# Moving keys, bias adds and value loads within the rounds of a decoder block kernel

## The chip, the core and the metric

The kernel runs on one core of one Trainium2 chip. A core has a matrix engine (TensorE, PE in the profile; its weight loads are shown as PEld), a vector engine (VectorE, DVE), a scalar engine (ScalarE, ACT), a general engine (GpSimd, POOL), and a queue engine (SyncE, SP) that here issues most of the transfers between device memory and on-chip memory. Each engine takes its instructions in the order of its own program and waits at an instruction until what it needs is there. The metric is the device time of one execution in microseconds; lower is better.

## The reference, cut to what matters

The kernel computes one decoder layer on 32 sequences ("blocks" in the code) of 256 tokens and 256 features, in float32, with a normalisation behind each of three parts:

```python
x = layernorm(x + self_attention(x))       # 16 heads, causal, keys and values of 72 latent columns
x = layernorm(x + cross_attention(x, ctx)) # 16 heads of 64, 120 context rows
x = layernorm(x + experts(x) + shared(x))  # 16 experts, each takes its best 32 tokens of a block

# self_attention
kv = x @ latent_w + latent_b                       # (256, 72): keys and values at once
q  = x @ Wd_w[h] + Wd_b[h]                         # (256, 72) for each head h
y  = softmax(causal(q @ kv.T / 4)) @ kv            # for each head
return concat(y) @ out_w + out_b
```

## The kernel before

**Stages.** Attention and the expert scores are computed in rounds, one per block, and fill the first 2100 us; the experts and the shared part follow and fill the rest. Round n (functions `first_half(n)` and `second_half(n)`) works on several blocks at once: the self attention scores of block n, the end of the self attention of block n - 1, cross attention of blocks n - 1 and n - 2, the last part of block n - 3, and the preparation of block n + 1 (load, transpose, keys, first queries, values). Block 0 is prepared in an opening part and run in `first_round()`.

**Quarters.** The 16 heads are worked in four groups of four, so a round has four quarters, each opened by `scores(n, g)`. For a group, TensorE computes scores into four accumulation banks; VectorE adds the causal mask (L479) and takes the maxima (L486); ACT takes exponentials and their sums (L493); VectorE inverts the sums (L503); POOL multiplies (L504); VectorE transposes in squares of 32 (L538, `turn`). After two groups `weigh(n, half)` multiplies with the values (pz, L564), the result z goes through device memory into zT (L586 to L592), and `latent_out` multiplies with the output weights (po) in the second quarter of the next round.

**The second quarter of round n** ends the self attention of block n - 1: `latent_out(n - 1)`, the moments and `norm_x1(n - 1)` (VectorE, L173, in two steps of 128 tokens), `turn_x1(n - 1)` (four transposes on TensorE, px1T, and one copy on VectorE, x1T, L195), then the cross queries of x1 (pqx). Between them stand `turn_x(n + 1)`, the third queries `queries(n, 2)` (pq), a part of the cross keys (pkx) in odd rounds or of the cross values (pvx) in even ones, and `keys(n + 1)`: two matmuls (pk), a copy with bias on ACT (kT, L377) and one on VectorE (kD, L378). In every fourth round, from round 6 on, `score` turns the gate's logits (pgT) ahead of pqx.

**The bias of the output projection** is added to x itself before the residual sum, by two adds on POOL (L366) at the end of `turn_x`. They read x after the transposes of x; their result is read by `latent_out` of that block, more than a round later.

**Values.** `values(n + 1)`, in the last quarter, transposes kT (pv), copies it (v) and writes it to device memory (vd). `place_values(n)`, in the second quarter of the next round, reads it back four times, one copy for each group of 32 partitions, into the one tile `vals`. That tile is read by both `weigh` of a block, the second of which stands in the first quarter of the round after; so the new values wait until `weigh(n - 1, 1)` is done.

**What sets the order.** The scope `tc.manual_schedule(engines=...)` keeps the order in which the code records instructions for the engines that it names: all engines in the opening part; TensorE, ACT and SP in `first_round`; TensorE, ACT, VectorE and POOL in the rounds. The engines that it does not name, SP in the rounds above all, are ordered by the scheduler, from the recorded order and its own estimates. Tiles of a pool with `bufs=k` rotate through k buffers, and a new tile waits until the last readers of the old one are done. Accumulation banks of the tag "r" rotate through six (`BUFS`), in the order in which they are asked for, whatever engine empties them; `cross_scores` has two banks of its own.

Of the kernel before, what the change touches and what calls it, by code (L numbers as in the profile page):

```python
# [26 lines left out]
P = 128  # L27
# [5 lines left out]
def decoder_kernel(  # L33
# [210 lines left out]

    kr = kp.tile([P, NG, T], F32, name="kr")
    nc.gpsimd.memset(kr, 0.0)

    vals = wp.tile([P, RB, TC, L], F32, name="vals")
    nc.gpsimd.memset(gw_sb, 0.0)

    xsms = [[cw.tile([P, HG, P], F32, name=f"xsm_{o}_{k}") for k in range(2)] for o in range(2)]
# [109 lines left out]
    def turn_x(s):  # L361
        st = states[s]
        st["xT"] = sp.tile([P, DC, T], F32, tag="xT", name=f"xT_{st['nm']}")
        transposed(st["xT"], (st["x"][:, 0, :], st["xb"]), f"pxT_{st['nm']}")
        for t in range(TC):
            nc.gpsimd.tensor_tensor(st["x"][:, t, :], st["x"][:, t, :], outb, ALU.add)  # L366

# [30 lines left out]

    def place_values(s):

        by_block = states[s]["v"].rearrange("(b i) t l -> i b (t l)", i=KB)
        for r in range(RB):
            nc.sync.dma_start(
                out=vals[r * KB : (r + 1) * KB].rearrange("i b t l -> i b (t l)"),
                in_=by_block,
            )
# [147 lines left out]
    def weigh(s, half):  # L554


        st = states[s]
        pzs = [bank("r", [L, TC, HH * KB], f"pz_{st['nm']}_{half}_{r}") for r in range(RB)]
        steps = [keys_of(r) for r in range(RB)]
        for i in range(len(steps[0])):  # L560
            for r in range(RB):
                t, b, at = steps[r][i]
                rows = slice(r * KB, (r + 1) * KB)
                nc.tensor.matmul(  # L564
                    pzs[r][:, t, :],
                    vals[rows, at[0], at[1], :],
                    st["d", t][rows, b].rearrange("p h i -> p (h i)"),
                    start=(i == 0),
                    stop=(i == len(steps[0]) - 1),
                )  # L570


        z = sp.tile([L, HH, T], F32, tag="z", bufs=1, name=f"z_{st['nm']}_{half}")
        blocks_of = z.rearrange("p h (b i) -> p b h i", i=KB)
        for r in range(RB):
            dst = blocks_of[:, r : 2 * RB - r : 2 * RB - 1 - 2 * r, :, :]
            src = pzs[r].rearrange("p t (h i) -> p t h i", i=KB)
            with urgent():
                if r % 2:
                    nc.vector.tensor_copy(dst, src)  # L580
                else:
                    nc.scalar.copy(dst, src)
        if half == 0:
            st["zT"] = sp.tile([P, ZC, T], F32, tag="zT", bufs=1, name=f"zT_{st['nm']}")
        rest = dram.tile([HH, LR, T], F32, tag=f"rest{half}", bufs=2, name=f"rest_{s}_{half}")
        nc.sync.dma_start(out=rest.rearrange("h l q -> l h q"), in_=z[LM:, :, :])  # L586
        for odd in range(2):
            nc.sync.dma_start(
                out=st["zT"][odd * LM : (odd + 1) * LM, half * HG : (half + 1) * HG, :],
                in_=z[0:LM, odd::2, :],  # L590
            )
        nc.sync.dma_start(  # L592
            out=st["zT"][half * LM : (half + 1) * LM, ZC - 1, :],
            in_=rest.rearrange("h l q -> (h l) q"),
        )
# [324 lines left out]
    def run(step, s, *args):  # L920
        if 0 <= s < B:
            step(s, *args)
# [16 lines left out]
    def first_round():  # L939

        scores(0, 0)
        queries(0, 1)
        turn_x(1)
        queries(0, 2)
        keys(1)
        weights(0, 0)
        scores(0, 1)
        query_rest(1)
        cross_keys(0, 0)
        turns(0, 0)  # L950
        weights(0, 1)
        out_weights(0)
        scores(0, 2)
        queries(0, 3)
        turns(0, 1)
        weights(0, 2)
        load_weights([(wv_sb, wv)])
        out_weights(1)
        weigh(0, 0)
        scores(0, 3)  # L960
        queries(1, 0)
        turns(0, 2)
        place_keys(1)
        cross_keys(0, 1)
        weights(0, 3)
        values(1)
        load_weights([(wq_sb, wq), (wo_sb, wo), (gw_sb[:, :, 0:E], gate_w)])
        turns(0, 3)

# [5 lines left out]
    def first_half(n):  # L975
        odd = n % 2 and n > 1
        run(load, n + 1)
        scores(n, 0)
        run(cross_scores, n - 2, 4, 0)
        run(moments_x2, n - 3)  # L980
        run(cross_values, n - 1, 0)
        peak(n, 0)
        if n == 1:
            queries(1, 1)
        run(norm_x2, n - 3)
        run(store_x2, n - 3)
        ex(n, 0, 0)
        run(cross_peak, n - 2, 4, 0)
        if n != 1:
            queries(n, 1)  # L990
        over(n, 0, 0)
        if odd:
            run(cross_values, n - 1, 1)
        ex(n, 0, 1)
        if odd:
            cross_keys(n // 2, 0, (0,))
        over(n, 0, 1)
        run(turn_x2, n - 3)
        run(cross_ex, n - 2, 4, 0, 0)
        run(cross_over, n - 2, 4, 0, 0)  # L1000
        weigh(n - 1, 1)
        if routed(n):
            route((n - 3) // BQ)
        turn(n, 0, 0)
        run(cross_weigh, n - 2, 0)
        run(cross_ex, n - 2, 4, 0, 1)
        run(cross_over, n - 2, 4, 0, 1)
        best_of(n, 0)

        scores(n, 1)  # L1010
        run(cross_scores, n - 2, 4, 1)
        place_values(n)
        peak(n, 1)
        ex(n, 1, 0)
        ex(n, 1, 1)
        run(cross_peak, n - 2, 4, 1)
        over(n, 1, 0)
        turn(n, 0, 1)
        over(n, 1, 1)
        run(cross_ex, n - 2, 4, 1, 0)  # L1020
        run(cross_ex, n - 2, 4, 1, 1)
        turn(n, 1, 0)
        both(cross_spread, n - 2, 4, 0)
        run(cross_over, n - 2, 4, 1, 0)
        latent_out(n - 1)
        moments_x1(n - 1)
        run(cross_over, n - 2, 4, 1, 1)
        run(turn_x, n + 1)
        queries(n, 2)
        if odd:  # L1030
            cross_keys(n // 2, 0, (2,))
        else:
            run(cross_values, n - 1, 1)
        norm_x1(n - 1)
        run(keys, n + 1)
        turn_x1(n - 1)
        if routed(n):
            score((n - 3) // BQ)
        if n % 2 == 0 and 2 <= n < B - 2:
            load_context(n // 2 + 1)  # L1040
        turn(n, 1, 1)
        cross_queries(n - 1, 0, 0)
        both(cross_spread, n - 2, 4, 1)
        cross_queries(n - 1, 0, 2)
        best_of(n, 1)

    def second_half(n):
        odd = n % 2 and n > 1
        scores(n, 2)
        cross_scores(n - 1, 0, 0)  # L1050
        cross_queries(n - 1, 4, 0)
        peak(n, 2)
        ex(n, 2, 0)
        cross_peak(n - 1, 0, 0)
        over(n, 2, 0)
        cross_queries(n - 1, 4, 2)
        ex(n, 2, 1)
        if odd:
            cross_keys(n // 2, 1, (0,))
        queries(n, 3)  # L1060
        over(n, 2, 1)
        cross_ex(n - 1, 0, 0, 0)
        cross_over(n - 1, 0, 0, 0)
        cross_ex(n - 1, 0, 0, 1)
        best_of(n, 2)
        weigh(n, 0)
        cross_over(n - 1, 0, 0, 1)
        turn(n, 2, 0)
        run(cross_weigh, n - 2, 4)
        turn(n, 2, 1)  # L1070

        scores(n, 3)
        cross_scores(n - 1, 0, 1)
        run(queries, n + 1, 0)
        peak(n, 3)
        ex(n, 3, 0)
        run(place_keys, n + 1)
        both(cross_spread, n - 1, 0, 0)
        cross_peak(n - 1, 0, 1)
        run(query_rest, n + 1)  # L1080
        over(n, 3, 0)
        ex(n, 3, 1)
        if odd:
            cross_keys(n // 2, 1, (2,))
        run(values, n + 1)
        over(n, 3, 1)
        cross_ex(n - 1, 0, 1, 0)
        turn(n, 3, 0)
        cross_over(n - 1, 0, 1, 0)
        cross_ex(n - 1, 0, 1, 1)  # L1090
        best_of(n, 3)
        turn(n, 3, 1)
        cross_over(n - 1, 0, 1, 1)
        both(cross_spread, n - 1, 0, 1)
        run(cross_out, n - 2)
        select_or_place(n)
# [52 lines left out]
    with tc.manual_schedule(engines=every):  # L1149
        warm_up(5)  # L1150
        load(0)
        first_weights()
        turn_x(0)
        order_first()
        warm_up(3)
        keys(0)
        queries(0, 0)
        place_keys(0)
        order_others()
        query_rest(0)  # L1160
        values(0)
        place_values(0)
        load_weights([(wk_sb, wk)])
        load_context(0)
        load_context(1)
    by_hand = {mybir.EngineType.PE, mybir.EngineType.Activation}
    with tc.manual_schedule(engines={*by_hand, mybir.EngineType.SP}):
# [307 lines left out]
```

## Time and profile before

| | |
|---|---|
| median of three runs | 3212.07 us (3207.21 to 3212.2) |
| profiled execution | 3211.46 us, span 3209.7 us |
| TensorE busy | 3129.1 us, 97% of the span |
| VectorE, ACT, POOL busy | 1754.4, 1360.9, 1071.3 us |
| TensorE's waits for x1T before pqx | 38.0 us in 31 waits |
| TensorE's waits for zT before po | 6.7 us in 12 waits |
| granted TensorE clock, mean | 0.997 |

A line of the timeline gives the start in us, the time from the first start to the last end of the instructions that were merged, the engine, the line of the code, the operation, the tile written and those read, the shape and the number of instructions; in square brackets stands the idle time of the engine before it, and what ended it. A line of the waits gives the engine and the line that waited, what it waited for, the total in us, the number of waits and the longest. A line of the table of stretches gives the stretch, its length, the busy time and number of instructions of each engine (PE, PEld, DVE, ACT, POOL), the granted share of TensorE's clock, the share of the DMA engines and GB/s. [...]

### The profile page before, as it was taken

The page shows a single profiled execution, that of the slowest core. Times are in us where ns is not written, and L with a number is a line of the kernel's source. Part 1 is how long each engine was busy: PE and PEld are TensorE (multiplying, and loading weights), DVE is VectorE, ACT ScalarE, POOL GpSimd, SP SyncE. Part 2 cuts the span into 40 slices and gives each one's busy share as a digit, 9 for nine tenths or more (in the row PEclk, how much of TensorE's full clock was granted, in tenths as well). Part 3 has the DMA queues.
Part 4 walks back from the last instruction along what each step waited for, and adds up shares of the span by engine and source line. Part 5 has one row for each costly group of instructions (what it writes and reads, how often), then busy time and mean ns, then how long its engine had stood idle before and what let it go on. Part 6 is the DMA issues. An engine that isn't in the chain of part 4 may idle for free.

```text
span 3209.7 us, 57226 instructions
## 1 busy us (share of the span) xinstructions
PE 3129.1 (97%) x21036; PEld 2276.3 (71%) x21036; DVE 1754.4 (55%) x3632; ACT 1360.9 (42%) x5181; POOL 1071.3 (33%) x955
## 2 busy tenths in 40 slices
PE   8999999999999999999999999999999999999999
PEld 6777777777777777777777777766566555665555
DVE  5667676677766767667666776644221233222133
ACT  4455555555555555555555555543111111111110
POOL 3333332333323333333333333333544202444400
PEclk9999999999999999999999999999999999999999
DMA  4333433343333333334333333333554422545421
GB/s 135 90 99 116 117 108 115 100 122 111 110 113 102 120 112 112 109 107 121 106 119 103 112 115 106 106 106 101 121 126 121 129 72 74 127 121 129 101 79 46
DMA packets 303008, 348.20 MB, mean 108 GB/s; under 512 B 47240, under 2 KB 263304, under 8 KB 302728
## 3 DMA queue, kind: packets, MB, share of 16 engines
q1 hardware_dynamic: 277936, 309.92, 32.3%
q0 software_dynamic: 24576, 34.62, 6.0%
q8 instruction: 167, 2.74, 0.4%
q14 instruction: 113, 0.93, 0.1%
q10 hardware_dynamic: 216, 0.01, 0.0%
HBM read 186.35 MB, written 120.32 MB: 96 GB/s over the span
## 4 chain that ended last, share of the span: by engine, by line
PE 86%; DVE 5%; DMA 3%; ACT 3%; issue 1%; POOL 1%; SPq 1%; POOLq 0%; ACTq 0%; DVEq 0%
PE po L201 11%; PE pz L564 8%; PE pqx L201 7%; PE pd L201 7%; PE pu L201 7%; PE pg L201 7%; PE pq L201 7%; PE pS L470 5%; PE pu_s L201 3%; PE pg_s L201 3%; PE pfo L201 3%; PE pc L775 3%; PE pvx L201 3%; PE pL L689 3%; PE pkx L201 3%; PE pS L458 3%
## 5 line engine op out<-in xcount | busy, mean ns | idle before, releaser
L504 POOL TENSOR_TENSOR sm<-sm,rs 128x512 f32<-128x512 f32 (+1 forms) x256 | 375.8, 1468 | 1000.4 <-DVE rs L503 1000.4
L493 ACT ACTIVATE sm<-sm,nmax 128x128 f32<-128x128 f32 (+1 forms) x1024 | 451.1, 445 | 117.9 <-DVE nmax L486 117.9
L493 ACT ACTIVATE xsm<-pL,nmax_x 128x120 f32<-128x120 f32 x1024 | 351.7, 365 | 2.2 <-DVE nmax_x L486 2.2
L504 POOL TENSOR_TENSOR xsm<-xsm,rs_x 128x480 f32<-128x480 f32 x256 | 252.7, 988 | 240.9 <-DVE rs_x L503 239.9
L1249 POOL DMA_INDIRECT acc<-eo,offs x128 | 200.8, 1569 | 335.7 <-DVE eo L1246 287.9
L479 DVE TENSOR_TENSOR sm<-pS,mask 128x384 f32<-128x384 f32 x512 | 247.4, 542 | 95.0 <-PE pS L470 94.9
L201 PE MATMUL pqx<-x1T,wq_sb 128*128 128x256 f32 x1024 | 237.8, 385 | 38.0 <-DVE x1T L195 38.0
L201 PE MATMUL pq<-xT,wd_sb 128*128 128x256 f32 x1152 | 273.7, 383 | 0.0
L564 PE MATMUL pz<-d,vals 32*72 32x256 f32 x4608 | 267.6, 379 | 3.5 <-DVE sm L479 1.8
L1320 DVE TENSOR_TENSOR hT<-gl,pu 128x512 f32<-128x512 f32 x128 | 87.9, 688 | 333.1 <-PE pu L201 180.9
L201 PE MATMUL po<-ow_sb,zT 128*128 128x256 f32 x1152 | 261.2, 383 | 7.0 <-DMA zT<-z 6.7
L538 DVE STREAM_TRANSPOSE d<-sm 128x512 f32<-128x512 f32 (+1 forms) x256 | 244.9, 957 | 23.9 <-POOL sm L504 23.8
L201 PEld LDWEIGHTS po<-ow_sb,zT 128*128 128x128 f32 x1152 | 214.3, 190 | 44.5 <-issue 12.4
L201 PEld LDWEIGHTS pq<-xT,wd_sb 128*128 128x128 f32 x1152 | 214.1, 190 | 43.7 <-issue 11.1
L201 PE MATMUL pg<-xeT,wg 128*128 128x512 f32 x512 | 240.8, 592 | 2.3 <-issue 2.3
L201 PEld LDWEIGHTS pqx<-x1T,wq_sb 128*128 128x128 f32 x1024 | 189.4, 190 | 72.6 <-DVE x1T L195 45.4
L201 PE MATMUL pu<-xeT,wu 128*128 128x512 f32 x512 | 240.7, 592 | 0.0
L167 POOL TENSOR_TENSOR rstd<-rstd,mhalf 128x2 f32<-128x2 f32 (+1 forms) x97 | 67.3, 693 | 507.3 <-DVE rstd L166 455.7
L564 PEld LDWEIGHTS pz<-d,vals 32*72 32x72 f32 x4608 | 177.4, 138 | 81.8 <-issue 11.4
L486 DVE TENSOR_REDUCE nmax<-sm 128x4 f32<-128x512 f32 (+1 forms) x256 | 231.6, 946 | 3.3
L201 PE MATMUL po<-wo_sb,cxT 128*128 128x256 f32 x1024 | 227.6, 380 | 0.0
L201 PE MATMUL pd<-wd,hT 128*128 128x256 f32 x1024 | 226.6, 379 | 0.0
(136 smaller groups left out, 5429.4 us busy)
## 6 DMA issues: line engine op xcount, KB each, us to landing
xd<-xb SPq DMA_DIRECT2D x120, 512.0 KB
xpt<-xd SPq DMA_DIRECT2D x480, 128.0 KB
zT<-z SPq DMA_DIRECT2D x128, 256.0 KB
wg<-in_wg_dram SPq DMA_DIRECT2D x32, 512.0 KB
wu<-in_wu_dram SPq DMA_DIRECT2D x32, 512.0 KB
wd<-in_wd_dram SPq DMA_DIRECT2D x32, 512.0 KB
vals<-vd SPq DMA_DIRECT2D x128, 72.0 KB
x<-in_x_dram SPq DMA_DIRECT2D x32, 256.0 KB
```

What stands on the lines that cost most here:

```text
L201: nc.tensor.matmul(acc, lhsT, rhs, start=(i == 0), stop=(i == n - 1))
L458: nc.tensor.matmul(pS[j][:, SEG[t]], st["q8"][rows, t * P : (t + 1) * P], kr[rows, g, 0 : (t + 1) * P], start=(t == TC - 1), stop=False,)
L470: nc.tensor.matmul(pS[2 * a + odd][:, SEG[t]], st["qT", g][rows, a, t * P : (t + 1) * P], k[rows, 0 : (t + 1) * P], start=False, stop=(t = ...
L479: nc.vector.tensor_tensor(sm[:, j, :], pS[j], mask, ALU.add)
L486: nc.vector.tensor_reduce(nmax, src, AX.X, ALU.max, negate=True)
L493: nc.scalar.activation(dst[:, a, :], src[:, a, :], AF.Exp, bias=nmax[:, a : a + 1], accum_out=rs[:, a, :],)
L504: nc.gpsimd.tensor_tensor(dst, dst, rs.to_broadcast(list(dst.shape)), ALU.mult)
L538: nc.vector.transpose(st["d", t][:, :, k * HG : (k + 1) * HG, :].rearrange("p b h i -> p h b i"), st["sm", g][:, :, SEG[t]].rearrange("p h ...
L564: nc.tensor.matmul(pzs[r][:, t, :], vals[rows, at[0], at[1], :], st["d", t][rows, b].rearrange("p h i -> p (h i)"), start=(i == 0), stop=( ...
L689: nc.tensor.matmul(pLs[odd][:, j, :], st["qxT", c0][rows, j, t * P : (t + 1) * P], pairs[s // 2]["kxT", c0][rows, j, s % 2, :], start=True ...
L775: nc.tensor.matmul(pc[odd * DH : (odd + 1) * DH, a, :], st["vx"][:, 2 * (c0 + j0 + a) + odd, :], st["xpt", c0][0:S2, :, odd * HG + j0 + a, :],
L1249: nc.gpsimd.indirect_dma_start(out=acc[b], out_offset=self.rows(b), in_=eo[:, k, :], in_offset=None, compute_op=ALU.add,)
```

## The change

Four things move; no computation is added or removed.

1. `turn_x1(n - 1)` comes before `keys(n + 1)` in the second quarter. TensorE's order becomes third queries, cross keys or values, px1T, pk, pqx; VectorE copies x1T before it makes kD.
2. The two bias adds leave `turn_x` and become `add_bias(n + 1)`, in the third quarter, on POOL behind the multiply of `over(n, 2, 1)` and ahead of the first cross multiply. For blocks 0 and 1 they stand in `first_round`.
3. `vals` becomes a tile of the pool `sp`, with two buffers, and `place_values(n + 1)` is recorded right behind `values(n + 1)` in the last quarter (for block 1 in `first_round`). On SP its four transfers now stand behind the `xpt` transfers of the first cross group instead of ahead of (three) and behind (one) the rest and zT transfers of the first quarter.
4. In the opening part, the cross key weights (`wk_sb`) and the first context are loaded ahead of the values of block 0. In `first_round`, the first queries of block 1 and the second half of the cross keys come ahead of `weigh(0, 0)`, and `values(1)` ahead of the exponentials of scores 3.

```diff
-    vals = wp.tile([P, RB, TC, L], F32, name="vals")
...
         transposed(st["xT"], (st["x"][:, 0, :], st["xb"]), f"pxT_{st['nm']}")
+
+    def add_bias(s):
+
+        st = states[s]
         for t in range(TC):
             nc.gpsimd.tensor_tensor(st["x"][:, t, :], st["x"][:, t, :], outb, ALU.add)
...
     def place_values(s):
 
+        vals = states[s]["vals"] = sp.tile([P, RB, TC, L], F32, tag="vals", name=f"vals_{s}")
...
-                    vals[rows, at[0], at[1], :],
+                    st["vals"][rows, at[0], at[1], :],
...
         out_weights(1)
+        queries(1, 0)
+        cross_keys(0, 1)
         weigh(0, 0)
         scores(0, 3)
-        queries(1, 0)
         turns(0, 2)
         place_keys(1)
-        cross_keys(0, 1)
+        add_bias(0)
+        add_bias(1)
+        values(1)
         weights(0, 3)
-        values(1)
+        place_values(1)
...
         run(cross_scores, n - 2, 4, 1)
-        place_values(n)
         peak(n, 1)
...
         norm_x1(n - 1)
+        turn_x1(n - 1)
         run(keys, n + 1)
-        turn_x1(n - 1)
...
         over(n, 2, 1)
+        run(add_bias, n + 1)
         cross_ex(n - 1, 0, 0, 0)
...
         run(values, n + 1)
+        run(place_values, n + 1)
         over(n, 3, 1)
...
         query_rest(0)
+        load_weights([(wk_sb, wk)])
+        load_context(0)
         values(0)
         place_values(0)
-        load_weights([(wk_sb, wk)])
-        load_context(0)
         load_context(1)
```

## The prediction

> **What bounds the kernel now.** I read the page's sums and its chain first, then TensorE's own waits, then the timeline of single rounds on all engines, and last the start of the program.
>
> ```profile
> span 3209.7 us, 57226 instructions
> PE 3129.1 (97%) x21036; PEld 2276.3 (71%) x21036; DVE 1754.4 (55%) x3632; ACT 1360.9 (42%) x5181; POOL 1071.3 (33%) x955
> PE 86%; DVE 5%; DMA 3%; ACT 3%; issue 1%; POOL 1%; SPq 1%; POOLq 0%; ACTq 0%; DVEq 0%
> ```
>
> TensorE is the bound: 3129.1 of 3209.7 us busy, 86% of the chain. No matmul is added or removed, so a gain can only come out of the 80 us in which TensorE idles. Its own waits say where they are:
>
> ```profile
> PE pqx L201 <- DVE x1T L195: 38.0, 31, 1.4
> PE po L201 <- DMA zT<-z: 6.7, 12, 1.6
> ```
>
> Almost half is one wait, once a round: the cross queries (pqx) wait for x1T, VectorE's copy of the turned x1. The timeline of a middle round (n = 7) shows what makes that copy late, the rows of TensorE first, then VectorE, POOL and ACT (start, us, engine, line):
>
> ```profile
> 477.81 1.78 PE L201 MATMUL pkx<-c,wk_sb 128*128 128x240 f32 x8
> 479.43 1.03 PE L201 MATMUL pk<-xT,lat_sb 128*96 128x256 f32 x4
> 480.29 0.66 PE L191 MATMUL px1T<-ident,x 128*128 128x128 f32 x4
> 482.25 1.56 PE L201 MATMUL pqx<-x1T,wq_sb 128*128 128x256 f32 x6 [1.30 <-DVE x1T L195]
> ...
> 478.55 1.80 DVE L173 TENSOR_SCALAR x<-r,mv,rstd 128x256 f32<-128x256 f32 x2 [0.15 <-POOL rstd L167]
> 480.99 0.48 DVE L378 TENSOR_SCALAR kD<-pk,latb 64x256 f32<-64x256 f32 x1 [0.65 <-ACT kT L377]
> 481.50 0.69 DVE L195 COPY x1T<-px1T 128x512 f32<-128x512 f32 x1
> ...
> 478.47 0.99 POOL L504 TENSOR_TENSOR xsm<-xsm,rs_x 128x480 f32<-128x480 f32 x1
> 479.42 1.51 POOL L366 TENSOR_TENSOR x<-x,outb 128x256 f32<-128x256 f32 x2
> ...
> 480.49 0.47 ACT L377 ACTIVATE kT<-pk,latb 96x256 f32<-96x256 f32 x1 [0.30 <-PE pk L201]
> ```
>
> Two things hold x1T. VectorE takes kD first, and kD waits for ACT's kT, which waits for the keys' matmuls (pk). And the two normalising steps at L173 take 1.06 and 0.81 us while POOL works beside them (the multiply of xsm, then the bias adds). The last round (n = 31) has no next block, so neither bias adds nor keys:
>
> ```profile
> 2077.82 1.38 DVE L173 TENSOR_SCALAR x<-r,mv,rstd 128x256 f32<-128x256 f32 x2 [0.73 <-POOL rstd L167]
> 2079.84 0.69 DVE L195 COPY x1T<-px1T 128x512 f32<-128x512 f32 x1 [0.64 <-PE px1T L191]
> 2080.59 1.59 PEld L201 LDWEIGHTS pqx<-x1T,wq_sb 128*128 128x128 f32 x8 [1.02 <-DVE x1T L195]
> ```
>
> Here the second step starts at 2078.80 and takes 0.40 instead of 0.81 us; x1T starts 0.64 us after its end, and pqx 0.75 after that. The norms of x2, with POOL idle, also take 0.40 each (0.73 for the pair at 454.93).
>
> **Keys behind the turn, bias adds moved** (rounds 1 to 30). In the new order TensorE goes pkx or pvx, px1T, pk, pqx; VectorE goes norm, x1T, kD; POOL has nothing behind the multiply of xsm. In the terms of round 31: the first step keeps its 1.06 (the multiply still overlaps it), the second starts 0.98 after the first and takes 0.40, then 0.64, 0.69 and 0.06. pqx can start 2.77 us after the norm begins. Round 7: 478.55 + 2.77 = 481.32 instead of 482.25, a gain of 0.93. TensorE is ready by then: the last transpose issues near 480.2, and pk's four matmuls, 0.86 us in all (479.43 to 480.29), end near 481.17. It idles some 0.6 us before px1T, with nothing put there, in place of 1.3 before pqx. The same arithmetic on each round's own rows: 0.93 in eleven odd rounds (10.2), 1.03 in seven even ones (7.2), 0.97 in the seven that also turn the gate's logits (6.8, held by TensorE), 1.0 in round 2, 0.41, 0.41 and 0.69 in rounds 11, 19 and 27, where the norm starts late (1.5), and 1.5 in round 1, where both steps fall from 0.81 to 0.40. Sum **28.2 us**. About 0.41 a round of it (12.3) hangs on the shorter norm alone.
>
> What is later: kT and kD by about 1 us. Behind kD on VectorE stand a turn (1.24) and two spreads (1.26), then the mask adds of the third scores. In round 7 the adds waited 3.19 us for TensorE, so a margin of nearly 2 us stays; in the routed round 14, with 3 us of gate work between, they waited 1.37, and by my count some 0.15 is left. kT's readers (kr's loads, query_rest, values) come a quarter or more later.
>
> **The bias adds in the third quarter** (1.51 us on POOL, behind the multiply of scores 2). They push one cross multiply: in round 7 it ran at 498.83 to 499.82; the multiply ahead ends at 497.95, the adds at 499.46, so it ends at 500.45, 0.6 later. Its reader, the spread, runs at 507.63. VectorE has reciprocals and copies out of PSUM there, which take the same with POOL beside them as without (0.68 for a z copy). Their transposes are long done, so the adds wait for nothing. Zero, covered by 7 us; without cover 1.5 a round.
>
> **Values in two buffers.** Four DMA issues a round leave the first half (three ahead of rest and zT: 1.55 us at 1061.68, one behind: 0.55) and stand behind xpt in the last quarter, ahead of the next xd. SP is idle there from 513.31 to 517.57, waiting for VectorE; the four take about 2.1 us, and vd, issued at 510.33, has 3 us to land (xd's own wait was 2.3). Nothing queued behind is later; if vd took 2 us more, xd and xpt would slip, with 8 us of cover before the cross values at 528.62. The gain: po's waits for zT, 4.6 us in rounds 3 to 31. rest's issue at 1063.34 came just behind the values' end (1063.23), so the issues cost little; their 216 KB ahead of rest may cost some. Between 0 and 4.6; rest to zT took 2.9 us there against 2.6 in a half without values (1034.66), so about **2**.
>
> **The first round** has its own sums; these are the rows:
>
> ```profile
> 28.59 6.17 PE L201 MATMUL pkx<-c,wk_sb 128*128 128x240 f32 x16 [3.37 <-DMA ow_sb<-in_out_w_dram]
> 52.96 3.40 PE L201 MATMUL pkx<-c,wk_sb 128*128 128x240 f32 x16
> 27.20:34.00 6.80, 5.41 (x14) 4.62 (x15) 3.55 (x5) 0.56 (x1) 1.21 (x1) 0.50 0.48 166
> 43.71 0.40 ACT L493 ACTIVATE sm<-sm,nmax 128x128 f32<-128x128 f32 x1 [3.72 <-DVE nmax L486]
> ```
>
> The first cross keys wait 3.37 us for wk (issued at 20.19, 7.90 in the chain) and then run at half clock (third row, 0.50 in the column behind the engines): 6.17 us against 3.40. With wk and the first context issued from 14.2, wk lands near 22, before TensorE gets there (25.2): 6.1 us sooner. But the gain does not stay. ACT's exponentials of scores 1 start 5.0 earlier (30.3, when their maxima are ready), those of scores 2 at 38.7 to 42.2. TensorE does queries(1, 0) and the second cross keys in between and reaches weigh(0, 0) at 37.8, where its fourth accumulation bank is the one that queries(1, 0) filled, and ACT empties that behind the exponentials of scores 2, near 43.1. So weigh starts 0.3 later than before (42.80), after 5 us of idling, and perhaps at half clock (up to 2.8 more by the first two rows), while 5.1 us of work that stood behind it is done. ACT's next exponentials then start 2 to 4 earlier. I take **2 us** gained, between 7 (no half clock, and the second such stretch, from 115.9 to 122.8, gone too) and a loss of 3.
>
> What decides is the clock: it was halved at 115.9 after a wait of 1.89 us within a stretch, and not in any later round before 2123, with waits of 1.1 to 1.4. [...]
>
> **The sum.** The profiled execution took 3211.46 us (span 3209.7), 0.6 under the median of 3212.07. 3211.5 - 28.2 - 2 - 2 = 3179.3; I say **3180**.
>
> **Rivals.**
> - *The norm stays long, or the moved keys bring less* (another stall on VectorE, transposes later). For it: the multiply of xsm stays beside the first step. Against it: round 31. Without the 0.41, 28.2 becomes 15.9: 3195 without the two small terms.
> - *The next wait swallows it*: VectorE, now idle for kT behind x1T, becomes late for the third scores. For it: 0.15 us of margin in routed rounds. Against it: nearly 2 in the others, and TensorE has 4 us of other matmuls behind those scores. With almost all lost: 3207.
> - *The small terms come out full*: 28.2 + 4.6 + 7: 3172.
> - *Slower: the clock*. The idle time moves in front of px1T, and those transposes may not count as work; if that stretch looked idle enough, the clock would be halved once a round. Price: 2.77 us (first two rows above) in 30 rounds, 83 us, so 3211 - 28 + 83 = 3266. It decides from about 1.9 us of idling in 3.4 us, as at 114.6; the old rounds had 1.5 and stayed at 1.00, the new ones have about 0.7. [...]
> - *The change does not do what it says*: excluded for the order: in the program as built, pk, kD, the adds and the values' loads stand in their new places in every round, and on TensorE nothing else moves after the first.
>
> **How the numbers follow.** Forecast 0.62 (3174 to 3188), long norm 0.16, swallowed 0.08, small terms full 0.09, clock 0.05. Range 3171 (all terms at their best: 39.8) to 3199 (15.9 and a first round 3 worse). Runs of this kernel lie between 3207.21 and 3212.2, so 0.2% (6.4 us) is about what can be told from no change. Faster 0.62 + 0.16 + 0.09 + 0.03 of the swallowed; same the rest of it; slower 0.05.
>
> **What would show it.** Right: pqx's wait for x1T near zero, a new wait of some 0.6 us of px1T for the norm; the pair at L173 at 1.38; a round of 65.7 where it was 66.7; no wait of the first pkx; one of 4 to 5 us inside the first pz. Wrong: pqx still waiting 0.5 or more (the norm), mask adds waiting for nothing in routed rounds and later matmuls waiting for VectorE (swallowed), a granted clock of 0.5 within the rounds (clock).

## The result, and the profile after

The changed kernel takes 3179.31 us (median of four runs, 3177.05 to 3182.65) against 3211.36 before: a ratio of 0.9904, interval 0.9886 to 0.9921. That is 0.7 from the forecast of 3180. That it came so near is luck: two of the terms behind it were wrong by 3 to 4 us and cancelled, so the terms are what this part is about.

The page of the changed kernel, its sums and the shares of the chain that ended last:

```profile
span 3180.9 us, 57119 instructions
PE 3133.5 (99%) x21036; PEld 2274.7 (72%) x21036; DVE 1745.4 (55%) x3632; ACT 1360.5 (43%) x5181; POOL 1066.6 (34%) x955
PE 90%; DVE 4%; ACT 2%; DMA 1%; POOL 1%; issue 1%; SPq 0%; POOLq 0%; ACTq 0%; DVEq 0%
```

TensorE does the same 21036 instructions and idles 47 us where it idled 81. Its waits (total, number, longest):

```profile
PE pS L461 <- DMA kr<-kT: 6.2, 2, 4.2
PE px1T L191 <- DVE x L173: 4.7, 15, 0.8
...
PE pz L567 <- ACT qT L438: 4.5, 1, 4.5
PE po L201 <- DMA zT<-z: 4.3, 5, 2.3
```

The 38 us of pqx for x1T are gone but for 0.8 in the last round; px1T's waits for the norm are 4.7, against 1.3 before. The third line is new, and so is the 4.2 of the first (the other wait in it, 2.0 in the opening part, was 1.8 before); both lie in the first round. Round 7, the timeline, TensorE's rows first, then VectorE's and POOL's (pk, two matmuls of the code, is x4 in these rows; px1T, four transposes, is x4 too):

```profile
472.45 1.78 PE L201 MATMUL pkx<-c,wk_sb 128*128 128x240 f32 x8
474.40 0.78 PE L191 MATMUL px1T<-ident,x 128*128 128x128 f32 x4 [0.17 <-DVE x L173]
475.02 1.03 PE L201 MATMUL pk<-xT,lat_sb 128*96 128x256 f32 x4
475.97 1.99 PE L201 MATMUL pqx<-x1T,wq_sb 128*128 128x256 f32 x8
...
473.19 1.39 DVE L173 TENSOR_SCALAR x<-r,mv,rstd 128x256 f32<-128x256 f32 x2 [0.15 <-POOL rstd L167]
475.22 0.69 DVE L195 COPY x1T<-px1T 128x512 f32<-128x512 f32 x1 [0.64 <-PE px1T L191]
476.59 0.48 DVE L380 TENSOR_SCALAR kD<-pk,latb 64x256 f32<-64x256 f32 x1 [0.67 <-ACT kT L379]
...
473.12 0.99 POOL L507 TENSOR_TENSOR xsm<-xsm,rs_x 128x480 f32<-128x480 f32 x1
```

From the norm's start to pqx are 475.97 - 473.19 = 2.78 us, the 2.77 that the forecast took from round 31; before it was 3.70. The pair at L173 takes 1.39.

Where the time of the two profiled executions (3211.46 and 3182.65 us) went, each stretch summed over the rounds from the starts of the instructions:

| stretch | forecast | measured |
|---|---|---|
| norm's start to pqx, rounds 1 to 31 | 28.2 | 27.7 |
| first po to norm's start (the waits for zT) | 2 | 5.1 |
| pqx to the next po, rounds 1 to 31 | 0 | 0.8 |
| program's start to the first po | +2 | -2.4 |
| behind the last po of the rounds | 0 | -2.3 |
| sum | 32.2 | 28.8 |

The loss behind the last po is one stretch of TensorE at half clock more (2115.2 to 2118.6 us); nine of the twelve profiles of this document have it and three do not. The row above it holds another such stretch, from 16.0 to 19.4 us. It lies ahead of the first cross keys (pkx), which begin at 26.93 here and at 25.07 to 25.40 in five of the six other kernels with the same loads in the opening part (the sixth, norm_clear: 26.70, without such a stretch). keys_only, with the loads of the kernel before, has a stretch at the same place (16.10), so some 1.7 of the 2.4 lost are put down to chance.

### The profile page after: what moved, and what is told of

Its sections match the earlier page's. It is cut to its first block, busy times and chain, and to the rows that moved or that the text cites. A ratio compares the mean times of both kernels' runs of the same rounds, so it can differ in the third digit from the quotient of the medians.

```text
span 3180.9 us, 57119 instructions
## 1 busy us (share of the span) xinstructions
PE 3133.5 (99%) x21036; PEld 2274.7 (72%) x21036; DVE 1745.4 (55%) x3632; ACT 1360.5 (43%) x5181; POOL 1066.6 (34%) x955
## 4 chain that ended last, share of the span: by engine, by line
PE 90%; DVE 4%; ACT 2%; DMA 1%; POOL 1%; issue 1%; SPq 0%; POOLq 0%; ACTq 0%; DVEq 0%
PE po L201 13%; PE pz L567 8%; PE pqx L201 7%; PE pd L201 7%; PE pu L201 7%; PE pg L201 7%; PE pq L201 7%; PE pS L473 5%; PE pvx L201 3%; PE pu_s L201 3%; PE pg_s L201 3%; PE pc L778 3%; PE pfo L201 3%; PE pL L692 3%; PE pS L461 3%; PE pkx L201 2%
## 5 line engine op out<-in xcount | busy, mean ns | idle before, releaser
L496 ACT ACTIVATION_READ_ACCUMULATOR xsm<-pL,nmax_x 128x1 f32 x1024 | 216.7, 212 | 0.0
```

What stands on the lines that cost most here:

```text
L496: nc.scalar.activation(dst[:, a, :], src[:, a, :], AF.Exp, bias=nmax[:, a : a + 1], accum_out=rs[:, a, :],)
```

## The experiments

Times are medians; the kernel before ran beside them at 3210.7 to 3211.9. "To pqx" is the sum of norm's start to pqx gained against the profile before, "to norm" that of first po to norm's start, "first po" the start of the first po in the profile (72.60 before). The last two columns also move by 1 to 3 us in kernels whose edit does not touch them.

| kernel | us | ratio (interval) | to pqx | to norm | first po |
|---|---|---|---|---|---|
| keys_only | 3197.10 | 0.9956 (0.9941 to 0.9971) | 15.2 | 0.0 | 69.86 |
| bias_only | 3210.84 | 0.9999 (0.9990 to 1.0008) | 0.2 | 1.2 | 71.84 |
| vals_only | 3205.91 | 0.9982 (0.9973 to 0.9991) | 0.3 | 6.0 | 71.72 |
| first_only | 3213.24 | 1.0010 (1.0001 to 1.0019) | -0.5 | 1.4 | 72.97 |
| rounds_only | 3176.99 | 0.9891 (0.9874 to 0.9907) | 27.7 | 6.4 | 73.67 |
| the change | 3179.31 | 0.9904 (0.9886 to 0.9921) | 27.7 | 5.1 | 75.00 |
| bank_only | 3173.17 | 0.9882 (0.9866 to 0.9899) | 27.7 | 6.3 | 66.83 |
| kr_only | 3178.67 | 0.9893 (0.9877 to 0.9910) | 27.7 | 5.8 | 71.09 |
| bank_fix | 3169.84 | 0.9869 (0.9853 to 0.9886) | 27.6 | 5.9 | 63.93 |
| norm_clear | 3165.73 | 0.9855 (0.9839 to 0.9872) | 42.0 | 5.9 | 74.20 |
| best | 3156.80 | 0.9829 (0.9812 to 0.9845) | 42.0 | 6.1 | 63.76 |

**keys_only: the turn ahead of the keys, nothing else** (on the kernel before, recorded as in part 1 of the change).

```diff
-        run(keys, n + 1)
         run(turn_x1, n - 1)
+        run(keys, n + 1)
```

> The kernel before with one edit: in each round x1 is turned (px1T) ahead of the next block's keys (pk) instead of behind them; bias adds, values' buffer and the first round as before. Theory (the keys and the shorter norm are two things that add): the second step at L173 keeps its 0.81 us, because POOL still adds the biases beside it, and the cross queries start 3.18 us after the norm begins (2.77 in the changed kernel, 3.7 to 3.8 before). That is 28.2 less 0.41 in 30 rounds, 15.9 us: about 3195.5. Rival (the order alone is what counts, the norm's length is hidden): 2.8 us from norm to cross queries and nearly all of the 28, about 3184. Rival (the wait moves to the next matmul): no gain, 3211.

3197.10 us. Round 7 in its timeline:

```profile
472.90 0.30 PE L191 MATMUL px1T<-ident,x 128*128 128x128 f32 x1 [0.16 <-DVE x L173]
473.55 0.55 PE L191 MATMUL px1T<-ident,x 128*128 128x128 f32 x3 [0.34 <-DVE x L173]
474.88 2.00 PE L201 MATMUL pqx<-x1T,wq_sb 128*128 128x256 f32 x8
...
471.70 1.79 DVE L173 TENSOR_SCALAR x<-r,mv,rstd 128x256 f32<-128x256 f32 x2
...
472.57 1.51 POOL L366 TENSOR_TENSOR x<-x,outb 128x256 f32<-128x256 f32 x2
```

pqx comes 474.88 - 471.70 = 3.18 us behind the norm's start, in every round but the first, those with gate logits (3.31) and the last. The pair stays at 1.79 with the bias adds beside its second step, and px1T's second half waits for that step. The theory of the expectation held: 15.2 us on this stretch, 15.9 expected.

**bias_only: the adds in the third quarter, nothing else** (for blocks 0 and 1 they stay behind the turn).

```diff
+        run(add_bias, n + 1)          # third quarter, behind over(n, 2, 1)
```

> The kernel before with one edit: the bias adds of the next x go to the third quarter (from block 2 on), keys still ahead of the turn. Theory (interaction): the second step at L173 falls from 0.81 to 0.40 us, but x1T then still stands behind kD, which waits for ACT's kT, so the cross queries start as late as before in nearly all rounds; only the rounds in which the norm starts late (11, 19, 27, 3.18 us from norm to cross queries before) and round 1 gain 0.4 each, 1 to 2 us: 3209 to 3211. Rival (the shorter norm is worth its 0.41 in every round by itself): 12.3 us, 3199. If the adds in the third quarter cost something there, 1.5 us a round would be 45 us: 3257.

3210.84 us, a ratio of 0.9999. Round 7:

```profile
481.44 1.78 PE L201 MATMUL pqx<-x1T,wq_sb 128*128 128x256 f32 x7 [1.36 <-DVE x1T L195]
...
477.74 1.39 DVE L173 TENSOR_SCALAR x<-r,mv,rstd 128x256 f32<-128x256 f32 x2
480.19 0.48 DVE L382 TENSOR_SCALAR kD<-pk,latb 64x256 f32<-64x256 f32 x1 [1.06 <-ACT kT L381]
480.70 0.69 DVE L195 COPY x1T<-px1T 128x512 f32<-128x512 f32 x1
```

The norm is 0.4 shorter and VectorE spends the 0.4 waiting for kT: 1.06 instead of 0.65, with x1T behind. pqx comes 3.70 behind the norm, as in the kernel before. So the shorter norm is worth nothing alone, and 27.7 - 15.2 - 0.2 = 12.3 us on this stretch when the order is changed too. The adds cost nothing that shows in the third quarter, as the forecast had it: the interval leaves room for 2.6 us, and 1.5 a round would have been 45.

**vals_only: the two value buffers, nothing else.**

```diff
+        vals = states[s]["vals"] = sp.tile([P, RB, TC, L], F32, tag="vals", name=f"vals_{s}")
...
+        run(place_values, n + 1)      # last quarter, behind values(n + 1)
```

> The kernel before with one edit: two buffers for the values and their loads issued in the last quarter of the round before. Theory: the time from the first po to the norm shrinks by what the changed kernel showed there, 5.1 us over all rounds, of which the listed waits of po for zT are some 3: about 3206.5. Rival (the recorded forecast, issues and shared bandwidth only in part): 2 us, 3209.5. Rival (the gain belongs to the other edits, or comes back in the last quarter through later loads of xd): 0, 3211.5.

3205.91 us, 2.9 to 8.7 less by the interval: as expected; the rival's 3209.5 lies less than 2 us outside. "To norm" tells them apart better: the four kernels with one buffer lie at 0.0 to 1.4, the eight with two at 5.1 to 6.4, and the means of the two groups are 5.3 apart. The waits for zT that the profile lists fell by 3.8 (rounds 1 to 31), yet 6.0 were gained. Most of the rest is in how a wait is listed. One po of the kernel before, in its timeline:

```profile
201.16 1.99 PE L201 MATMUL po<-ow_sb,zT 128*128 128x256 f32 x8
203.91 1.10 PE L201 MATMUL po<-ow_sb,zT 128*128 128x256 f32 x4 [0.75 <-DMA zT<-z]
```

The same po in vals_only:

```profile
199.96 3.72 PE L201 MATMUL po<-ow_sb,zT 128*128 128x256 f32 x16
```

Sixteen matmuls take 3.72 and eight 1.99, so one adds 0.216 and the last of a row 0.26 more, which the next overlaps when nothing is waited for. The second half could have started at 201.16 + 8 x 0.216 = 202.89 and started at 203.91: 1.02 late, listed as 0.75. In eight rounds 0.19 to 0.27 of the gain lies outside the listed waits, together 1.9 of the missing 2.1.

**first_only and rounds_only: the first round's edits alone (the diff, and values(1) and the loads as in part 4 of the change), and all but these.**

```diff
         turns(0, 1)
         weights(0, 2)
         load_weights([(wv_sb, wv)])
         out_weights(1)
+        queries(1, 0)
+        cross_keys(0, 1)
         weigh(0, 0)
-        queries(1, 0)
...
-        cross_keys(0, 1)
```

> The kernel before with one edit: the opening and the first round of the changed kernel (cross key weights and first context ahead of the first values; the second block's queries and cross keys behind the third scores), all later rounds as before. Theory: the wait of the first cross keys (3.37 us) goes, a wait of 4.5 us for ACT inside the first weigh and one of 4.2 us for kr at the second block's first scores come, the clock is halved once more than before, and the first po of block 0 comes 2.4 us later: about 3214, give or take the 2.8 us that one stretch of half clock later in the program is worth. Rival (the recorded forecast): 2 us earlier, 3209.5; in that case the 2.4 belong to the other edits.

> The changed kernel with the opening and first round of the kernel before (keys behind the turn, bias adds in the third quarter and two value buffers stay). Theory (the first round loses 2.4 us and the rest adds up): norm to cross queries 2.77 us in each round, first po at the kernel before's place, about 3176.5 to 3177. Rival (the first round's edits gain, as forecast): 3181 to 3182. Rival (the two half-clock stretches after 2090 us are of these edits and not of the first round): they stay, 3179.

3213.24 and 3176.99 us: the first round's edits lose 0.3 to 6.1 us by the interval of the one, and 2.3 by the medians of the changed kernel and the other (whose intervals overlap). In the profile of first_only, which has no stretch of half clock at 16.0, the first po comes only 0.4 later than before. So a gain of 2 is excluded; the size of the loss is not settled. The waits in the changed kernel's first round:

```profile
26.93 3.40 PE L201 MATMUL pkx<-c,wk_sb 128*128 128x240 f32 x16
...
45.01 6.38 PE L567 MATMUL pz<-d,vals 32*72 32x256 f32 x65 [4.53 <-ACT qT L438]
...
58.95 1.66 PE L461 MATMUL pS<-kr,q 32*128 32x256 f32 x16 [4.24 <-DMA kr<-kT]
```

And SP's own rows there:

```profile
52.62 0.28 SPq L589 DMA_DIRECT2D rest<-z  x1
52.95 1.31 SPq L591 DMA_DIRECT2D zT<-z  x2
55.34 0.49 SPq L595 DMA_DIRECT2D zT<-rest  x1
55.87 2.61 SPq L385 DMA_DIRECT2D kr<-kT  x4
```

The first cross keys no longer wait, and the wait inside the first pz is there with the length that the forecast gave it. The wait for kr is the one it missed. SP issues kr behind the rest and zT of the first weigh, and in the kernel before the second block's queries and cross keys (5.1 us on TensorE) stood between that weigh and the scores that read kr. With these moved ahead, no matmuls are left to cover the load.

**bank_only, kr_only and bank_fix: the two covers (work that hides a wait) given back, one at a time and together.** bank_only records the queries and cross keys ahead of `weights(0, 2)`, so that ACT empties their banks before the exponentials of scores 2; kr_only loads three of the four groups of kr ahead of `weigh(0, 0)`; bank_fix does both.

```diff
         turns(0, 1)
+        queries(1, 0)                 # bank_only, bank_fix
+        cross_keys(0, 1)
         weights(0, 2)
         load_weights([(wv_sb, wv)])
         out_weights(1)
-        queries(1, 0)                 # bank_only, bank_fix
-        cross_keys(0, 1)
+        place_keys(1, range(3))       # kr_only, bank_fix
         weigh(0, 0)
         scores(0, 3)
         turns(0, 2)
-        place_keys(1)
+        place_keys(1, range(3, NG))
```

> The changed kernel with the first round put in another order: the second block's queries and cross keys ahead of the third weights (so that ACT empties their banks before it takes the exponentials of scores 2), and three of the four groups of kr of block 1 loaded ahead of the first weigh's rest and zT on SP. Theory (two covers were lost): the wait of 4.53 us for ACT's qT inside the first pz and the 4.2 us of pS for kr go, and with them the half-clock stretches between 43 and 64 us: 5 to 8 us less than the changed kernel, 3171 to 3174. Rival (something else is late there, the exponentials' own chain or the values): the waits turn up at the next matmul, within 2 us of 3179.

> The changed kernel with the second block's queries and cross keys ahead of the third weights, so that ACT empties their banks before the exponentials of scores 2; the kr loads stay behind the first weigh's rest and zT. Theory (two separate covers): the wait of 4.5 us for ACT inside the first pz goes, the wait of 4.2 us for kr at the second block's first scores stays, since the kr loads follow the first weigh wherever it goes; with one half-clock stretch less 5 to 6 us of the 9.5 that both edits gave: about 3174. Rival (the bank is all): kr's wait goes too, 3170. Rival (the kr loads are all): the freed time turns up as a longer wait for kr, 3179.

> The changed kernel with three of the four kr groups of block 1 loaded ahead of the first weigh's rest and zT; the second block's queries and cross keys stay behind the third weights. Theory (two separate covers): the wait of 4.5 us inside the first pz stays, the one of 4.2 us for kr goes, with one half-clock stretch less 4 to 5 us of the 9.5: about 3175. Rival (the bank is all): the kr wait stays or moves to the next matmul, 3179. Rival (the kr loads are all): 3170.

3169.84, 3173.17 and 3178.67 us. TensorE's row for the second block's scores in bank_only:

```profile
50.53 1.66 PE L461 MATMUL pS<-kr,q 32*128 32x256 f32 x16 [4.23 <-DMA kr<-kT]
```

Its row for pz in kr_only:

```profile
43.32 6.50 PE L567 MATMUL pz<-d,vals 32*72 32x256 f32 x65 [4.53 <-ACT qT L438]
...
62.84 5.08 PE L567 MATMUL pz<-d,vals 32*72 32x256 f32 x64 [1.70 <-DVE d L541]
```

Each edit removes the wait it was made for and leaves the other as long as it was: the two are separate. What follows differs. The first po comes 8.2 us earlier than in the changed kernel in bank_only, 3.9 in kr_only and 11.1 in bank_fix; 1.5 to 1.9 of each lie ahead of both edits, with the changed kernel's stretch of half clock at 16.0. Counted from the start of the first cross keys, 6.3, 2.2 and 9.5 are left. In kr_only 1.7 of the 4.2 turns into a wait of the next pz for VectorE's transpose of the weights; by the medians it gained 0.6, and the intervals do not tell it from the changed kernel, so the expected 4 us are not confirmed. Together the median falls by 9.5, more than the 5 to 8 expected: no stretch of half clock is left before 105 us, and two of the three that went lie where the two waits were.

**norm_clear: nothing on POOL beside the norm.** On the changed kernel, the last cross multiply two blocks back (VectorE's reciprocal, POOL's multiply) is recorded behind the norm.

```diff
-        run(cross_over, n - 2, 4, 1, 1)
...
         run(norm_x1, n - 1)
+        run(cross_over, n - 2, 4, 1, 1)
```

> The changed kernel with one more edit: the last cross multiply of scores 3 two blocks back (VectorE's reciprocal and POOL's multiply of xsm) is recorded behind the norm of x1, so that POOL does not multiply beside the first step of the norm. Theory (POOL's work beside it is what makes the step at L173 take 1.06 instead of 0.40 us): both steps take 0.40, px1T starts 0.6 us earlier in each round, its wait goes, and the rounds lose some 0.5 to 0.6 each, 15 to 18 us: 3161 to 3164. Rival (the first step is long for another reason, its place behind the statistics): it keeps 1.06, 3179. Rival (the later multiply becomes late for its spread): waits of the cross values, above 3179.

3165.73 us, 13.6 less by the medians and 14.2 on the stretch to pqx, short of the 15 to 18 expected. Round 7:

```profile
468.55 1.78 PE L201 MATMUL pkx<-c,wk_sb 128*128 128x240 f32 x8
470.17 0.60 PE L191 MATMUL px1T<-ident,x 128*128 128x128 f32 x4
470.61 1.03 PE L201 MATMUL pk<-xT,lat_sb 128*96 128x256 f32 x4
471.56 1.99 PE L201 MATMUL pqx<-x1T,wq_sb 128*128 128x256 f32 x8
...
469.29 0.74 DVE L173 TENSOR_SCALAR x<-r,mv,rstd 128x256 f32<-128x256 f32 x2 [0.21 <-POOL rstd L167]
...
470.26 0.99 POOL L507 TENSOR_TENSOR xsm<-xsm,rs_x 128x480 f32<-128x480 f32 x1 [1.00 <-DVE rs_x L506]
```

Both steps take 0.4, the pair 0.74: POOL's work beside them was what made them long (in all 128 steps of x1 and x2 with nothing on POOL beside them, 0.40 to 0.42). The gain of 0.50 in this round is less than the 0.65 by which the pair shrank, because now TensorE is the limit: none of its rows here waits, and pqx starts when pk has been issued.

**best: bank_fix and norm_clear together.**

> The changed kernel with both further edits (the first round's order, and the cross multiply behind the norm). Theory: they lie in different places and add up: 5 to 8 and 15 to 18 us, 3153 to 3159. Rival: if only the one or the other holds, 3172 or 3162.

3156.80 us (four runs within 0.62 us of each other), 0.9829 of the time before (0.9812 to 0.9845). The two gains add: 9.5 and 13.6 make 23.1, and 22.5 were measured.

## Why the prediction was right, step by step

- **Keys behind the turn, shorter norm: 28.2, measured 27.7.** Right, and for its reason. Round 31 was the model of the new order, and the traces show its 2.77 us in nearly all rounds. The split was right too: 12.3 were to hang on the shorter norm, and the runs of the two halves alone leave 12.3 that only both together give. The difference of 0.5 is in the rounds with gate logits (2.90). TensorE idles before px1T less than the 0.6 said: 0.17 as listed, 0.33 by the starts (1.95 from pkx to px1T here, 1.62 in norm_clear).
- **Bias adds in the third quarter: 0, measured 0** (bias_only, to within 3 us).
- **Values in two buffers: 2 taken, between 0 and 4.6; measured 5.1, and 6.0 alone.** The mechanism was right and the term mis-sized, its upper bound probably too (5.3 between the kernels with one buffer and with two). The bound was the sum of the listed waits; by the rows of po a stop costs TensorE about 0.26 more than the list says. And the choice of the middle was wrong: most of the waits went (3.6 of 4.6 in rounds 3 to 31 of vals_only), not just what the issue times explain: in the rows of round 3, rest is issued 3.35 us ahead of po in the kernel before and 3.66 in vals_only, 0.3 apart, and the stop was 1.02. What the values' transfers cost the others on their way was not taken apart further.
- **The first round: 2 gained, measured 0.3 to 6.1 lost (first_only); 2.4 in the profiled execution, some 1.7 of them put down to chance.** The step that failed is "while 5.1 us of work that stood behind it is done". The weigh did start late with 4.5 us of idling and half clock behind it, as said (43.30 in first_only, 43.32 in kr_only against the 43.1 worked out, with the first scores and queries at full clock). But the work that was moved away had covered the loads of kr, and 4.2 of the 5.1 came back as the wait for them; with it the forecast's sum would have been 2 - 4.2, a loss of 2.2. The forecast listed what the moved matmuls wait for, and not what had been waiting in their shadow.
- **Rivals.** The long norm is refuted by round 7, the swallowed gain by the 0.8 of the stretch behind pqx, the halved clock by the granted clock of 1.00 in the rounds (no stretch of half clock between 125.2 and 2091.3 us). The small terms did not come out full: the values did, the first round lost. A round's length, as a line of the table of stretches:

```profile
400.00:467.00 67.00, 66.93 (x556) 52.67 (x555) 48.59 (x102) 39.12 (x164) 22.70 (x21) 1.00 0.39 113
```

- **The total** came out within 1 us by luck: 3 too little for the values met 4 too much for the first round, and the profiled execution, with the two stretches of half clock named above, took 3182.65. The rounds shrank by 1.1 us on average (66.46 to 65.35, rounds 1 to 30 from po to po), where 1.0 was forecast. The levels of 66.7 and 65.7 named there cannot be read off a single round: rounds go from 62.4 to 67.9 before and from 61.6 to 67.2 after.

## What to carry to other kernels

When work is moved out of a place, list what ran in its shadow there (loads behind it on a queue, copies on other engines), and not only what it will wait for in its new place: here 5.1 us of moved matmuls uncovered 4.2 us of loads. Two causes of one late start do not add when one hides behind the other: neither the order nor a shorter norm could be priced without saying what the other did, and an engine's own row behind the wait (here kD waiting for kT) shows which one holds. A wait listed for a pipelined engine can fall short of what the stop costs (0.75 listed, 1.02 lost).

## What the runs showed of the hardware

**VectorE beside POOL.** A step of the norm (128x256 float32, on-chip memory to on-chip memory) takes 0.40 to 0.42 us with POOL idle, 0.81 beside the bias add and 1.06 beside the multiply of xsm. norm_clear and bias_only agree that it is POOL's work that costs: with the multiply recorded behind the norm, or the add moved to the third quarter, the step that stood beside it takes 0.4. The step does not stand still until POOL's row is over: in round 7 of the changed kernel the multiply begins at 473.12, ahead of the step, and ends at 474.11 by its row, so a step that began its work then would have ended 0.40 later, 1.32 after its start, and it took 1.06. What in POOL's work slows it is not shown.

**Half clock begins on a grid.** All 45 stretches of half clock in the twelve profiles (those at the very end of the program left out) begin on a grid of 3.413 us, whose phase differs from run to run, and last one to three steps of it (in the changed kernel those at 15.97 and 121.78 last 3.413 each and begin 31 steps apart). All but three follow a step in which TensorE was busy for half of the time or less (the three: 0.52, 0.56, 0.66). Near one half it can go either way. The wait of 1.89 us at the third scores of round 1 in vals_only (columns: stretch, length, busy us of PE, PEld, DVE, ACT and POOL, granted clock, share of the DMA engines, GB/s):

```profile
110.20:113.60 3.40, 1.51 (x13) 1.16 (x11) 3.40 (x7) 2.81 (x12) 0.00 (x0) 1.00 0.25 77
113.60:117.00 3.40, 2.52 (x33) 2.10 (x34) 1.12 (x5) 3.40 (x18) 2.27 (x2) 1.00 0.53 193
```

And the same place in first_only:

```profile
112.80:116.20 3.40, 1.51 (x23) 1.20 (x23) 2.38 (x6) 3.40 (x16) 1.04 (x1) 1.00 0.40 162
116.20:119.60 3.40, 2.85 (x18) 2.13 (x14) 1.48 (x4) 3.37 (x20) 2.45 (x2) 0.50 0.54 166
```

TensorE is busy for 1.51 us in both, and only the second is followed by half clock. One program gets more or fewer such stretches from run to run: the mean granted clock of the changed kernel's four runs is 0.995 to 0.998. That this is what moves the first po, 69.86 to 73.67 us in five profiles with the same order of the first round on TensorE (the kernel before, keys_only, bias_only, vals_only, rounds_only), is argued and not shown, since no program was profiled twice. A forecast of a first round to 2 us was finer than this scatter.
